# Rotary products of Strassen's queries issued one by one behind score tiles' maxima

## The chip, the cores and the metric

The kernel runs on one core of one Trainium2 chip. The metric is the device time of one execution in microseconds (us), as the median of the runs shown; the profile is of one further execution. The engines are called PE (matrix products), DVE (vector), ACT (scalar functions), POOL (GpSimd) and SP (issues most DMAs).

## The reference

One decoder layer on a sequence of 1024 rows of width 512, all in float32: attention with 32 query heads and 8 key/value heads of width 128, rotary positions and a causal mask, an output projection, layer normalisation, then a gated network of inner width 1792 and a second normalisation.

```python
q = (x @ wq).reshape(B, T, H, HD).transpose(0, 2, 1, 3)     # H = 32, HD = 128
k = (x @ wk).reshape(B, T, KV, HD).transpose(0, 2, 1, 3)    # KV = 8
v = (x @ wv).reshape(B, T, KV, HD).transpose(0, 2, 1, 3)
q = q * cos + _rotate_half(q) * sin
k = k * cos + _rotate_half(k) * sin
...
scores = jnp.einsum('bhtd,bhsd->bhts', q, k) * (1.0 / np.sqrt(HD))
scores = jnp.where(mask, scores, -jnp.inf)
att = jax.nn.softmax(scores, axis=-1)
out = jnp.einsum('bhts,bhsd->bhtd', att, v)
...
x = _layernorm(x + out @ wo, axis=-1)
x = _layernorm(x + ffn(x), axis=-1)
```

## The kernel before

The work runs over eight groups g. A group is one key/value head with its four query heads. Its 1024 rows are cut into eight row tiles i of 128 rows, taken in the order 7, 1, 5, 3, 4, 2, 6, 0: odd row tiles in the first half of a group, even ones in the second. Each row tile is cut again into four score tiles t = 4i to 4i + 3. A score tile holds 32 rows of all four heads and (t + 1) x 32 keys, so s_28 to s_31 are the long ones with which a group begins, and s_0 to s_3 the short ones with which it ends. The text calls the passage from s_3 of one group to s_28 of the next a turn.

**A score tile** (function scores). PE multiplies the rotated queries by the keys into one of two PSUM pairs (pool ps_s). DVE adds the mask and takes the row extreme in one instruction (L503; the profile calls its result low; the text calls it the tile's maximum). ACT takes the exponential (L517), which frees the PSUM pair. DVE takes the reciprocal of the sums (L521), ACT scales (L522), and DVE transposes in blocks (L525). After a row tile's fourth score tile, SP issues 16 DMAs (gather, L575) that complete the transposition; only then can PE form o, the weights times v (class Late, which also runs the output projection y of a pair of row tiles, with the sums os that POOL forms at L651 to L654 and the accumulation on DVE at L672).

**The next group's projections** (class Early) fill PE between score tiles: keys, values and queries of g + 1, in units of one 512-wide matmul. Most pairs of query heads, 13 of 16, are projected with Strassen's seven products (project_two, in the order 1, 2, 6, 5, 3, 7, 4), whose weight sums POOL forms ahead in weigh (L248 to L251). Four results come out: c11 and c12 are the odd row tiles of the pair's first and second head, c21 and c22 the even ones. The three other pairs (the list PLAIN) are projected directly.

**The rotation** (rotate) of one result takes three products on DVE, two of half the partitions with sin (L381) into a buffer rope_b, of which there are two, and one with cos in place (L387), and one add on POOL (L390). In project_two all four follow at once when the result is complete. The queries of odd rows of g + 1 must be complete, for all four heads, before s_28 of g + 1; those of even rows are first read at the fifth row tile.

**The order.** A scheduler orders instructions on each engine by the order in which they are written and by when it deems them ready; PE's order is the written one. The written order comes from a planner that counts PE's units: function run fills the time after each score tile with Late's steps that are due and else with Early's steps. For the groups 0 to 5 Early must be done EARLIER score tiles before a group's end:

```python
pace = early.total * min(1, passed / (slots - EARLIER))
must = early.total - MOST * max(0, slots - EARLIER - done)
```

The o of a row tile counts as ready to be used COPY = 5 units after its last matmul, so that y of that pair is written later. In the first group the residual rows x are loaded into sums (load_x, L292 to L300), with two memsets and a subtraction on POOL for each of four pairs of row tiles, and each weight block is turned into a difference on POOL (difference, L256) after its first use.

Of the kernel before, what the change touches and what calls it, by code (L numbers as in the profile page):

```python
# [35 lines left out]
P = 128  # L36
# [8 lines left out]
NT = T // P  # L45
# [40 lines left out]
STEP = 3.5  # L86
LAG = 7

EARLIER = 2

LEAST = 2

# [2 lines left out]
def kernel(  # L95
# [55 lines left out]
    def piece(name):  # L151
        return cp.tile([P, T], F32, tag="c", name=name)
# [27 lines left out]
    with ExitStack() as att:  # L180
# [108 lines left out]
        def load_x(k):  # L289


            for n in range(2):  # L292
                i = ORDER[2 * k + n]
                to = sums[k][:, 2:4, :] if n else sums[k][:, 1:7:5, :]
                src = x_in[i * P : (i + 1) * P, :]
                nc.sync.dma_start(to, src.rearrange("p (n f) -> p n f", n=2))
            a1, _, _, a5, a6, a7, a3 = (sums[k][:, n, :] for n in range(7))
            nc.gpsimd.memset(a1, 0.0)
            nc.gpsimd.memset(sums[k][:, 4:6, :], 0.0)
            nc.gpsimd.tensor_tensor(a3, a3, a5, ALU.subtract)  # L300
# [41 lines left out]
        nc.vector.tensor_tensor(s2, s1, a11, ALU.subtract)  # L342
        nc.vector.tensor_tensor(s4, a12, s2, ALU.subtract)

        def values(g, even):

            if g not in vs:
                vs[g] = piece(f"v{g}").rearrange("p (j f) -> p j f", j=NT)
            pv = mbank(f"v_ps{g}_{even}")
            for j in range(NT // 2):  # L350
                for c, (w, x) in enumerate(operands(wvs[g], even)):
                    matmul(
                        pv[:, j * HD : (j + 1) * HD],
                        lhsT=x[:, j * P : (j + 1) * P],
                        rhs=w,
                        start=(c == 0),
                        stop=(c == NC - 1),
                    )
                if j == NT // 2 - 1:
                    nc.scalar.copy(  # L360
                        vs[g][:, 1 - even :: 2, :], pv.rearrange("p (j f) -> p j f", f=HD)
                    )
                    if even:
                        load_wv(g + 1)
                    else:
                        difference(wvs[g])
                yield NC * HD / W

        def alike(t, dst):

            return t.rearrange("p (n q) -> p n q", q=dst.shape[-1])

        def rotate(dst, src, even, name):

            ts = slice(even * W, (even + 1) * W)
            b = ap.tile([P, W], F32, tag="rope_b", name=f"{name}_b{even}")


            def swapped():
                for to, of in ((slice(0, 64), slice(64, P)), (slice(64, P), slice(0, 64))):  # L380
                    nc.vector.tensor_tensor(  # L381
                        alike(b, dst)[to], src[of], alike(sin[:, ts], dst)[of], ALU.mult
                    )

            if src is dst:
                swapped()
            nc.vector.tensor_tensor(dst, src, alike(cos[:, ts], dst), ALU.mult)  # L387
            if src is not dst:
                swapped()
            nc.gpsimd.tensor_tensor(dst, dst, alike(b, dst), ALU.add)  # L390

        def project(dst, w, even, name):

            ps = mbank(f"{name}_ps{even}")
            for c, (w_c, x_c) in enumerate(operands(w, even)):
                matmul(ps, lhsT=w_c, rhs=x_c, start=(c == 0), stop=(c == NC - 1))
                if c < NC - 1:
                    yield 1
            rotate(dst, alike(ps, dst), even, name)
            if not even:  # L400
                difference(w)
            yield 1

# [7 lines left out]

        def project_queries(g, head, even):
            dst = queries(g, even)[:, :, head, :]
            yield from project(dst, wqs[g * REP + head], even, f"q{g}_{head}")
            if even and head % 2:
                for h in (head - 1, head):
                    load_wq((g + 1) * REP + h)
                weigh((g * REP + head) // 2 + 1)

        def project_two(g, n):  # L420


            b11, b21, b22, u1, u2, u3, u4 = sums_of[g * 2 + n]
            u = f"{g}_{n}"
            v = ap.tile([P, W], F32, tag="v", bufs=1, name=f"qv{u}")
            c11, c12, c21, c22 = (
                queries(g, even)[:, :, 2 * n + h, :] for even in range(2) for h in range(2)
            )
            v_q = alike(v, c11)
            ps = {}  # L430
            products = (
                (1, b11, a11), (2, b21, a12), (6, u2, s2), (5, u1, s1), (3, b22, s4),
                (7, u3, s3), (4, u4, a22),
            )
            for k, w, x in products:
                ps[k] = mbank(f"q{u}_p{k}")
                q = alike(ps[k], c11)
                for c in range(NC // 2):
                    matmul(
                        ps[k], lhsT=w[:, c], rhs=x[:, c], start=c == 0, stop=c == NC // 2 - 1  # L440
                    )
                    if c < NC // 2 - 1:
                        yield 1
                if k == 1:
                    nc.scalar.copy(v, ps[1])
                elif k == 2:
                    nc.vector.tensor_tensor(c11, q, v_q, ALU.add)
                    rotate(c11, c11, 0, f"q{u}_0")
                elif k == 6:
                    nc.vector.tensor_tensor(v, ps[6], v, ALU.add)  # L450
                elif k == 5:
                    nc.vector.tensor_tensor(c12, q, v_q, ALU.add)
                elif k == 7:
                    nc.vector.tensor_tensor(v, ps[7], v, ALU.add)
                    nc.vector.tensor_tensor(c22, alike(ps[5], c22), v_q, ALU.add)
                    rotate(c22, c22, 1, f"q{u}_1")
                elif k == 4:
                    nc.vector.tensor_tensor(c21, q, v_q, ALU.add)
                    rotate(c21, c21, 1, f"q{u}_0")
                    for h in range(2):  # L460
                        load_wq((g + 1) * REP + 2 * n + h)
                    weigh(g * 2 + n + 1)
                else:
                    nc.vector.tensor_tensor(c12, q, c12, ALU.add)
                    rotate(c12, c12, 0, f"q{u}_1")
                yield 1

        def projections(g):
# [15 lines left out]
        def scores(g, t, kT, x):  # L484

            nonlocal last_of_all
            n, i, b = (t + 1) * Q, t // B, t % B
            full = (i + 1) * P  # L490
            u = f"{g}_{t}"
            s = pair(f"s{u}")
            for k0 in range(0, n, W):
                k1 = min(n, k0 + W)
                matmul(
                    s[:, k0:k1],
                    lhsT=queries(g, i % 2 == 0)[:, i // 2 * B + b].rearrange("p h q -> p (h q)"),
                    rhs=kT[:, k0:k1],
                    start=True,
                    stop=True,  # L500
                )
            low = stat("low", f"low{u}")
            nc.vector.tensor_tensor_reduce(  # L503
                out=s[:, :n],
                in0=s[:, :n],
                in1=mask[:, T - n :],
                scale=1.0,
                scalar=MASKED,
                op0=ALU.add,
                op1=ALU.min,  # L510
                accum_out=low,
            )
            p = piece(f"p{u}")
            if n < full:
                nc.gpsimd.memset(p[:, n:full], 0.0)  # L515
            total = stat("total", f"total{u}")
            nc.scalar.activation(  # L517
                p[:, :n], s[:, :n], AF.Exp, bias=low, scale=-1.0, accum_out=total
            )
            share = stat("share", f"share{u}")  # L520
            nc.vector.reciprocal(share, total)  # L521
            last_of_all = nc.scalar.activation(p[:, :n], p[:, :n], AF.Copy, scale=share)  # L522
            if x is None:
                return p[:, :full]
            nc.vector.transpose(  # L525
                x[:, :, :, b, :].rearrange("p b j q -> p j b q"),
                p[:, :full].rearrange("p (j b k) -> p j b k", b=B, k=Q),
            )
# [326 lines left out]
        for g in range(KV):  # L855
# [21 lines left out]
            passed = 0.0  # L877
            due = now
            for p, i in enumerate(ORDER):
                if g == KV - 1 and p == 1:  # L880
                    load_wo(g)
                x = turned(g, p, i)
                unturned = []
                for b in range(B):
# [337 lines left out]
```

## Time and profile before

| | us |
|---|---|
| median of 3 runs | 1336.13 (1335.11 to 1337.87) |
| profiled execution | 1334.31 |
| its span, first to last instruction | 1332.4 |
| PE busy | 1283.2 |
| DVE busy | 830.4 |
| ACT busy | 466.1 |
| POOL busy | 421.2 |
| mean clock granted to PE | 0.986 of full |

A row of the timeline reads: start in us from the span's begin, length in us, engine, line and operation, output<-inputs, the shape, how many records were merged (a matmul in float32 leaves two), and in brackets the engine's idle time before it and what ended it. A row of the waits reads: total us, how many times, the longest. Line numbers such as L503 are those of the kernel before.

### The profile page before, as it was taken

How to read it: one execution, taken by the hardware profiler on the slowest of the kernel's cores; microseconds unless marked ns; L12 is line 12 of the kernel's file. 1: busy time of each engine (PE TensorE's matmuls, PEld its weight loads, DVE VectorE, ACT ScalarE, POOL GpSimd, SP SyncE). 2: the span in 40 equal slices, each digit the busy share in tenths (PEclk: the TensorE clock that was granted, in tenths of full speed). 3: DMA queues.
4: the chain of work that ended last, by engine and by line, in shares of the span. 5: the costliest groups of instructions: out<-in, count | busy, mean ns of one | idle time of the engine just before them, and what ended most of it. 6: DMA issues, size and time to landing. Idle time of an engine off the chain costs nothing. (4 is left out here: it accounts for less than half of the span.)

```text
span 1332.4 us, 13958 instructions
## 1 busy us (share of the span) xinstructions
PE 1283.2 (96%) x4046; PEld 719.8 (54%) x4046; DVE 830.4 (62%) x1665; ACT 466.1 (35%) x924; POOL 421.2 (32%) x631
## 2 busy tenths in 40 slices
PE   8999989998998999899999999999999999999998
PEld 3565555655564656465556565654655644444445
DVE  5567766776678667867676768686755564344122
ACT  0443344434443444344434344445445111111000
POOL 6233333332333233413332323252320534532000
PEclk9899989998999999999999999999999999999999
DMA  7243215342534243334333433433444611100000
GB/s 244 52 117 93 71 44 144 89 101 53 137 88 106 56 127 93 89 75 118 83 92 82 127 80 81 112 90 89 118 102 103 187 32 47 48 27 5 16 24 24
DMA packets 104235, 115.52 MB, mean 87 GB/s; under 512 B 19040, under 2 KB 79200, under 8 KB 104160
## 3 DMA queue, kind: packets, MB, share of 16 engines
q1 hardware_dynamic: 103152, 112.67, 32.4%
q10 hardware_dynamic: 1008, 1.97, 0.4%
q8 instruction: 33, 0.54, 0.2%
q14 instruction: 42, 0.34, 0.1%
HBM read 37.23 MB, written 2.10 MB: 30 GB/s over the span
## 5 line engine op out<-in xcount | busy, mean ns | idle before, releaser
L517 ACT ACTIVATE p<-s,low 128x928 f32<-128x928 f32 (+31 forms) x256 | 178.9, 699 | 463.7 <-DVE low L503 445.5
L134 PE MATMUL s<-kT,queries 128*128 128x512 f32 (+15 forms) x768 | 281.0, 476 | 37.2 <-ACT p L517 31.6
L134 PE MATMUL o<-moved,v 128*128 128x512 f32 x550 | 256.7, 598 | 0.2 <-issue 0.2
L134 PEld LDWEIGHTS s<-kT,queries 128*128 128x128 f32 x768 | 144.1, 193 | 193.2 <-issue 151.1
L525 DVE STREAM_TRANSPOSE turned<-p 128x1024 f32<-128x1024 f32 (+7 forms) x244 | 186.3, 774 | 98.2 <-ACT p L522 68.9
L503 DVE CUSTOM_DVE_ANT_0 s<-s,mask 128x928 f32<-128x928 f32 (+31 forms) x256 | 178.5, 698 | 66.4 <-PE s L134 65.7
L522 ACT ACTIVATE p<-p,share 128x928 f32<-128x928 f32 (+31 forms) x256 | 187.0, 735 | 91.1 <-DVE share L521 91.1
L134 PEld LDWEIGHTS o<-moved,v 128*128 128x128 f32 x550 | 101.9, 191 | 96.8 <-issue 90.9
L390 POOL TENSOR_TENSOR queries<-queries,q_b 128x512 f32<-128x512 f32 x64 | 83.6, 1306 | 153.4 <-DVE queries L387 69.9
L521 DVE RECIPROCAL share<-total 128x1 f32<-128x1 f32 x256 | 41.1, 161 | 113.6 <-ACT p L517 111.2
L134 PE MATMUL y<-wo,oT 128*128 128x256 f32 x428 | 106.1, 384 | 0.0
L134 PE MATMUL q_p<-blocks,wq 128*128 128x512 f32 x208 | 98.9, 594 | 0.0
L515 POOL MEMSET p<- 128x96 f32 (+2 forms) x192 | 26.3, 151 | 220.7 <-DVE turned L525 205.9
L381 DVE TENSOR_TENSOR q_b<-queries,sin 64x512 f32<-64x512 f32 x104 | 93.5, 899 | 3.0
L134 PEld LDWEIGHTS y<-wo,oT 128*128 128x128 f32 x428 | 81.9, 194 | 24.4 <-issue 10.9
L134 PE MATMUL q_p<-blocks,uq 128*128 128x512 f32 x156 | 75.9, 594 | 0.0
L134 PEld LDWEIGHTS v_ps<-wv,blocks 128*128 128x128 f32 x512 | 64.1, 194 | 13.9 <-issue 11.2
L672 DVE TENSOR_TENSOR sums<-y,sums 128x512 f32<-128x512 f32 x112 | 67.9, 610 | 4.5 <-PE y L134 3.6
L134 PE MATMUL v_ps<-wv,blocks 128*128 128x128 f32 x512 | 64.5, 277 | 0.4 <-POOL p L515 0.4
L134 PE MATMUL f<-wd,hT 128*128 128x512 f32 (+1 forms) x162 | 64.8, 545 | 0.0
L134 PE MATMUL k_ps<-blocks,wk 128*128 128x512 f32 x128 | 62.8, 607 | 2.0 <-POOL wk L256 2.0
L134 PEld LDWEIGHTS q_p<-blocks,wq 128*128 128x128 f32 x208 | 38.7, 190 | 38.6 <-issue 35.4
(183 smaller groups left out, 1504.0 us busy)
## 6 DMA issues: line engine op xcount, KB each, us to landing
moved<-turned SPq DMA_DIRECT2D x112, 128.0 KB, 2.4
moved<-turned SPq DMA_DIRECT2D x128, 112.0 KB, 2.2
moved<-turned SPq DMA_DIRECT2D x112, 96.0 KB, 2.1
moved<-turned SPq DMA_DIRECT2D x112, 80.0 KB, 2.1
wq<-wq SPq DMA_DIRECT2D x32, 256.0 KB, 2.9
wo<-wo SPq DMA_DIRECT2D x32, 256.0 KB, 3.4
moved<-turned SPq DMA_DIRECT2D x128, 64.0 KB, 2.0
moved<-turned SPq DMA_DIRECT2D x128, 48.0 KB, 1.9
```

The source lines that it names most:

```text
L134: tc.keep_in_program_order(nc.tensor.matmul(*args, **kw))
L381: nc.vector.tensor_tensor(alike(b, dst)[to], src[of], alike(sin[:, ts], dst)[of], ALU.mult)
L390: nc.gpsimd.tensor_tensor(dst, dst, alike(b, dst), ALU.add)
L503: nc.vector.tensor_tensor_reduce(out=s[:, :n], in0=s[:, :n], in1=mask[:, T - n :], scale=1.0, scalar=MASKED, op0=ALU.add, op1=ALU.min, acc ...
L515: nc.gpsimd.memset(p[:, n:full], 0.0)
L517: nc.scalar.activation(p[:, :n], s[:, :n], AF.Exp, bias=low, scale=-1.0, accum_out=total)
L521: nc.vector.reciprocal(share, total)
L522: last_of_all = nc.scalar.activation(p[:, :n], p[:, :n], AF.Copy, scale=share)
L525: nc.vector.transpose(x[:, :, :, b, :].rearrange("p b j q -> p j b q"), p[:, :full].rearrange("p (j b k) -> p j b k", b=B, k=Q),)
L672: pin(nc.vector.tensor_tensor(to, out, to, ALU.add))
```

## The change

Three things are edited. In project_two the calls of rotate become rotate_later: each puts three pieces of work, the two half products and the cos product with its add, into one of two queues (chores), one for odd and one for even row tiles. The function chore takes the next piece, odd rows' rotations first and each rotation to its end, and scores calls it once behind each tile's maximum, twice for the short tiles of row tile 0. Before a group's first score tile what is left for odd rows is written out; before its fifth row tile, everything. EARLIER goes from 2 to 3. In the first group the memsets and subtractions of load_x become begin_sums, written ahead of the first four row tiles one pair at a time, and the four weight differences of the first queries are written ahead of the first row tile.

```diff
-EARLIER = 2
+EARLIER = 3
...
+        def begin_sums(k):
             a1, _, _, a5, a6, a7, a3 = (sums[k][:, n, :] for n in range(7))
             nc.gpsimd.memset(a1, 0.0)
             nc.gpsimd.memset(sums[k][:, 4:6, :], 0.0)
...
+        chores = deque(), deque()
+
+        def rotate_later(dst, even, name):
+
+            ts = slice(even * W, (even + 1) * W)
+            b = []
+
+            def half(to, of):
+                if not b:
+                    b.append(ap.tile([P, W], F32, tag="rope_b", name=f"{name}_b{even}"))
+                nc.vector.tensor_tensor(
+                    alike(b[0], dst)[to], dst[of], alike(sin[:, ts], dst)[of], ALU.mult
+                )
+
+            def whole():
+                nc.vector.tensor_tensor(dst, dst, alike(cos[:, ts], dst), ALU.mult)
+                nc.gpsimd.tensor_tensor(dst, dst, alike(b[0], dst), ALU.add)
+
+            low, high = slice(0, 64), slice(64, P)
+            chores[even].extend([lambda: half(low, high), lambda: half(high, low), whole])
+
+        def chore(behind=None):
+
+
+            nonlocal current
+            if current is None:
+                current = next((c for c in chores if c), None)
+            if current is None:
+                return False
+            with tc.issue_after(behind) if behind is not None else ExitStack():
+                current.popleft()()
+            if len(current) % 3 == 0:
+                current = None
+            return True
...
-            if not even:
+            if not even and diff:
                 difference(w)
...
                 elif k == 2:
                     nc.vector.tensor_tensor(c11, q, v_q, ALU.add)
-                    rotate(c11, c11, 0, f"q{u}_0")
+                    rotate_later(c11, 0, f"q{u}_0")
...
-                    rotate(c22, c22, 1, f"q{u}_1")
+                    rotate_later(c22, 1, f"q{u}_1")
...
-                    rotate(c21, c21, 1, f"q{u}_0")
+                    rotate_later(c21, 1, f"q{u}_0")
...
-                    rotate(c12, c12, 0, f"q{u}_1")
+                    rotate_later(c12, 0, f"q{u}_1")
...
-            nc.vector.tensor_tensor_reduce(
+            extreme = nc.vector.tensor_tensor_reduce(
...
+            for _ in range(2 if i == 0 else 1):
+                chore(extreme.ins)
...
             for p, i in enumerate(ORDER):
+                while p % 4 == 0 and (chores[0] or (p and chores[1])):
+                    chore()
                 if g == KV - 1 and p == 1:
                     load_wo(g)
+                if g == 0 and p == 0:
+                    for a in range(REP):
+                        difference(wqs[a])
+                if g == 0 and p < NT // 2:
+                    begin_sums(p)
```

More of the change, by code (lines that the diff above doesn't have):

```diff
@@ L383, in swapped, with project @@
                     )
-            if src is dst:
-                swapped()
             nc.vector.tensor_tensor(dst, src, alike(cos[:, ts], dst), ALU.mult)
-            if src is not dst:
-                swapped()
+            swapped()
             nc.gpsimd.tensor_tensor(dst, dst, alike(b, dst), ALU.add)
-        def project(dst, w, even, name):
+        chores = deque(), deque()
[22 more added lines that the diff above has]
+            if len(current) % 3 == 0:
+                current = None
+            return True
+        def project(dst, w, even, name, diff=True):
             ps = mbank(f"{name}_ps{even}")
@@ L413, in project_queries @@
             dst = queries(g, even)[:, :, head, :]
-            yield from project(dst, wqs[g * REP + head], even, f"q{g}_{head}")
+            yield from project(dst, wqs[g * REP + head], even, f"q{g}_{head}", g > 0)
             if even and head % 2:
```

## Prediction

> **What bounds the kernel now.** I read the page's busy table first, then the waits of PE, then PE's timeline around the long waits, then DVE and POOL over the same stretch.
>
> ```profile
> PE 1283.2 (96%) x4046; PEld 719.8 (54%) x4046; DVE 830.4 (62%) x1665; ACT 466.1 (35%) x924; POOL 421.2 (32%) x631
> ```
>
> PE is the bound: 1283.2 of 1332.4 us busy, so 49.2 us idle, and the change adds and removes no matmul. It can win only what lies in those 49.2 us (and in PE's slow-clock time), and loses whatever idle time it creates. PE's waits (total us, times, longest us):
>
> ```profile
> PE s L134 <- ACT p L517: 31.6, 15, 5.0
> PE s L134 <- POOL queries L390: 5.0, 1, 5.0
> ```
>
> A score tile's product waits until the exponential of the tile two before has emptied its PSUM pair: 31.6 us. PE's timeline (start, us, ..., idle before) shows where:
>
> ```profile
> 157.61 0.30 PE L134 MATMUL s<-kT,queries 128*128 128x32 f32 x2
> 157.75 1.10 PE L134 MATMUL o<-moved,v 128*128 128x512 f32 x2
> ...
> 166.31 0.49 PE L134 MATMUL s<-kT,queries 128*128 128x128 f32 x2
> 166.63 1.89 PE L134 MATMUL y<-u,os 128*128 128x256 f32 x8
> 173.48 3.43 PE L134 MATMUL s<-kT,queries 128*128 128x512 f32 x4 [4.96 <-ACT p L517]
> 176.71 1.57 PE L134 MATMUL y<-wo,oT 128*128 128x256 f32 x4
> 178.11 1.03 PE L134 MATMUL y<-wo,os 128*128 128x256 f32 x4
> ```
> ```profile
> 303.35 3.43 PE L134 MATMUL s<-kT,queries 128*128 128x512 f32 x4 [4.96 <-ACT p L517]
> ```
> ```profile
> 562.73 2.68 PE L134 MATMUL s<-kT,queries 128*128 128x512 f32 x4 [4.10 <-ACT p L517]
> ```
> ```profile
> 689.92 1.79 PE L134 MATMUL s<-kT,queries 128*128 128x512 f32 x4 [1.96 <-ACT p L517]
> ```
>
> These are the turns from one group to the next, between the four short tiles s_0 to s_3 and the long s_28: six turns, idle 4.96, 4.96, 5.22 (0.27 and 4.95 at 433), 4.10, 1.96, 1.97 (at 817), in all 23.2 us. After a long one the same form of s_28 takes 3.43 instead of 1.79 and the next y 1.57 (1.03 warm): the clock has fallen. That loses 2.2, 2.1, 1.7 and 1.7 us at the first four. A turn now costs 31 us over all six. The cause is on DVE:
>
> ```profile
> 165.62 0.14 DVE L503 DVE_READ_ACCUMULATOR2_ANT low<- 128x1 f32 x1
> 165.78 2.20 DVE L381 TENSOR_TENSOR q_b<-queries,sin 64x512 f32<-64x512 f32 x2
> ...
> 170.04 2.56 DVE L381 TENSOR_TENSOR q_b<-queries,sin 64x512 f32<-64x512 f32 x2
> 172.52 0.25 DVE L503 CUSTOM_DVE_ANT_0 s<-s,mask 128x96 f32<-128x96 f32 x1
> ```
>
> Between the maxima of s_1 and s_2 lie 6.8 us of rotary products. And POOL:
>
> ```profile
> 159.75 0.72 POOL L651 TENSOR_TENSOR os<-oT 128x256 f32<-128x256 f32 x1
> ...
> 161.91 1.18 POOL L654 TENSOR_TENSOR os<-oT,os 128x256 f32<-128x256 f32 x1
> 165.04 1.26 POOL L390 TENSOR_TENSOR queries<-queries,q_b 128x512 f32<-128x512 f32 x1 [1.95 <-DMA moved<-turned]
> 166.26 1.18 POOL L248 TENSOR_TENSOR uq<-wq,wq 128x256 f32<-128x256 f32 x1
> ...
> 169.33 1.06 POOL L251 TENSOR_TENSOR uq<-wq,uq 128x256 f32<-128x256 f32 x1
> 170.35 1.70 POOL L390 TENSOR_TENSOR queries<-queries,q_b 128x512 f32<-128x512 f32 x1
> ```
>
> The add at 165.04 is the last one that s_28 needs (odd tiles, second head); it stands ahead of weigh's four subtractions (L248 to L251), so POOL is not what PE waits for here.
>
> **The change: rotations behind maxima.** Counts stay: 52 rotations of three DVE products and one POOL add. What changes is their place. In the instruction order of the changed program DVE has one product (two at the short tiles) behind each maximum, odd tiles' rotations first. Between the maxima of s_1 and s_2 only one half product and a reciprocal remain, 1.3 us for 6.8. That takes away the wait shown. But the same order shows two new things at every one of the six turns.
>
> First, EARLIER = 3: the projections are all spent one tile sooner. PE has the output product o of tile row 2, the two matmuls of the pair's last product (4), then s_1, s_2, s_3 and s_28 with nothing between them. Before, 2.6, 1.7 and 1.7 us of q_p and y matmuls stood there; they now stand behind s_28 and can't cover a wait of s_28.
>
> Second, the add of that second odd rotation now comes late: on POOL it stands behind os (L651 to L654), the add of the first odd rotation, and weigh's four. POOL runs in order, so s_28 waits for all of it. From the end of o (158.85 in the trace of before) on: 0.90 to the first os (ACT's copy between, 159.75), os 3.34 (to 163.09), add 1.26, weigh 4.13 (166.26 to 170.39), add 1.26 to 1.70 (both rows are there; I take the middle, 1.48), and 0.05 to PE's start (the add that ended at 36.05 and PE's start at 36.10). Sum 11.16 us. PE has in that time 1.72 for two matmuls and 0.17 + 0.20 + 0.32 for s_1 to s_3: 2.41. Idle 8.75 us a turn. At the first turn weigh's first subtraction stands before the other add; the sum is the same.
>
> Is DVE later than that? From the same zero: tile 27's transposition ended 6.94 after its product began (152.67 to 159.61), 0.65 of it a product of v that now stands behind; the o ends 6.8 after that start (1.5 for s_27, five matmuls of 0.86, s_0, one more), so the transposition ends at -0.5, v takes 0.65 and the maximum of s_0 0.30, done at about 0.5. Then 0.68 (c22), 1.12 (cos beside a busy POOL), 1.15 (half of 2.2 to 2.4), 0.16, 0.67, 0.30, 0.36 (s_1), 1.15, 0.16, 0.35 (s_2), 1.12 (cos of the odd rotation): 7.7. POOL reaches the add at 9.6, so POOL decides by 1.9 us. The exponential of s_2 is done by 7.2. Without weigh in the way the add would end at 9.1, idle 6.7.
>
> **The clock.** The row first: after idle of 4.96, s_28 and y lost 2.2 us; after 1.96, none (1.79 for s_28). The Trainium skill, "TensorE: Matmul & The Clock Gate", Part 1, says PE falls to half clock after an idle window of about 3.4 us and comes back only after a busy one, the windows running freely. It speaks against this change: two turns that pay nothing today would pay, and the penalty would be half of 3.4 to 6.8 us, 1.7 to 3.4 a turn, 10 to 20 in all; by the row, 6 x 2.2 = 13. I use the row, and the rule's ends for the range.
>
> New cost of the turns: 6 x (8.75 + 2.2) = 65.7, less today's 31: +34.7 us.
>
> **Elsewhere in a group.** The wait that moves on: the transposition of tile 31 (L525) now has a half product in front of it, 1.15 us later at most, and its 16 DMAs are what o of row 7 waits for. In the trace it ended at 197.99; 16 issues of 0.63 and 2.4 to land give 210.4, the o matmul began at 212.75. The new order puts that o one tile later, so it stays covered. In short tiles 4 to 7 PE has 2.2 to 2.5 us each where DVE needs about 2.2; between 0 and +6 over six groups, below nothing -1.9, which is all that waits of 0.3 to 0.6 in mid group hold. I take +1. On SP one wq load of a pair (0.5 us to issue, and a wait for PE) moves ahead of row 6's gather; that gather has over 10 us to spare before its o, as s_28 to s_30, y and k_ps now come first. ACT keeps its work.
>
> **GpSimd's first group.** In the built order the eight memsets and four subtractions of sums stand where they stood; only the first wq difference (L256) passes the memsets. POOL then waits 3.75 us for wo until 17.32 anyway, which covers it; the 5.01 us at 36.10 and 1.99 at 20.54 on PE stay, since every add and difference around them keeps its place. Without that cover it would cost the 2.9 us of memsets. I take 0; a gain of more than 2 is excluded, as nothing on POOL in front of those adds goes away. The other three differences keep their place too.
>
> **Sum.** 1332.4 + 34.7 + 1 = 1368.1 span. The profiled execution took 1334.31, 1.9 above its span, and stands 1.8 under the median of 1336.13: 1371.8.
>
> **The rivals.** (a) Faster: the tile chain alone decides. If the odd adds land early, s_28 waits only for the exponential of s_2; with half products at the undisturbed 0.69 that is t = 5.8 on the scale above, idle 3.4 and little slow clock: 6 x 3.4 = 20.4 for 31, about -10.6 us, 1325.5. It decides from the point where idle and slow clock stay under 5.2 us a turn, that is, the last add landed by about 7.6. For it: DVE's gap shrinks from 6.8 to 1.3. Against it: POOL's queue shows 8.7 us of work in front of that add after 0.9. 8 in 100.
>
> (b) Slower, but less: os or weigh run earlier than I place them, and DVE's 9.1 decides: 6 x (6.7 + 2.2) - 31 = +22, 1359. 10 in 100.
>
> (c) Slower, and more: longer slow clock (3.4) and o waiting for gathers in mid group: 6 x (9.5 + 3.4) - 31 + 6 = +52, 1389. 10 in 100.
>
> (d) The change doing nothing, as its GpSimd part does in the built order: gains and losses at the turns cancel. The different PE order at all six turns speaks against it: 2 in 100.
>
> The likeliest case has 70 in 100. A measurement of this kernel tells 0.2%, 2.7 us, from no change. Faster 0.08, same 0.02, slower 0.90. The range: the main case runs from +28 to +49 (add 1.26 or 1.70, clock 1.7 to 3.4, mid group -2 to +6), and (b) and part of (c) are taken in: 1352 to 1391.
>
> **What would show it.** Right: at the six turns PE's s_28 waits for POOL queries, 8 to 10 us in two pieces around s_3 (the first for ACT p), in all 48 to 60 us; s_28 at 3 us or more; busy sums unchanged; PE idle near 85 us. Wrong: PE's wait for ACT p gone with no wait for POOL in its place; or the wait for POOL near 4, then weigh ran ahead; or new waits of o for DMA.

## The result, and the profile after

The changed kernel takes 1380.51 us (median of 4 runs, 1379.3 to 1381.53); the kernel before, run beside it, 1335.62 (4 runs, 1334.97 to 1337.87). The ratio is 1.0333, interval 1.0315 to 1.0351: 45 us slower. The profiled execution took 1381.53 with a span of 1379.8, 47.4 longer than the span before, at a mean granted PE clock of 0.971 (0.986 before).

The page's busy table of the changed kernel:

```profile
PE 1289.6 (93%) x4046; PEld 722.3 (52%) x4046; DVE 823.5 (60%) x1665; ACT 466.8 (34%) x924; POOL 423.8 (31%) x631
```

The work is the same, instruction for instruction in number. PE is idle for 1379.8 - 1289.6 = 90.2 us, 41.0 more than before, and busy 6.4 longer. Its waits (us in all, times, longest):

```profile
PE s L134 <- POOL queries L411: 43.2, 6, 7.3
PE s L134 <- ACT p L558: 20.9, 17, 2.5
PE s L134 <- POOL queries L391: 6.7, 1, 6.7
PE q_p L134 <- DVE sums L713: 6.3, 5, 1.4
```

The first row is new: score products wait for the rotated queries that POOL's add writes (L390 of before is L411 here in project_two's rotations, and L391 in the direct ones). It stands at six places, once in each turn. PE's timeline at the first turn (start, us, idle before in brackets), and then the matching lines of the second:

```profile
160.08 1.10 PE L134 MATMUL o<-moved,v 128*128 128x512 f32 x2
161.02 1.88 PE L134 MATMUL q_p<-blocks,uq 128*128 128x512 f32 x4
162.74 0.58 PE L134 MATMUL s<-kT,queries 128*128 128x64 f32 x4
165.84 0.77 PE L134 MATMUL s<-kT,queries 128*128 128x128 f32 x2 [2.52 <-ACT p L558]
173.50 3.46 PE L134 MATMUL s<-kT,queries 128*128 128x512 f32 x4 [6.88 <-POOL queries L411]
176.75 3.28 PE L134 MATMUL y<-wo,oT 128*128 128x256 f32 x8
179.86 1.03 PE L134 MATMUL y<-u,oT 128*128 128x256 f32 x4
...
302.81 0.49 PE L134 MATMUL s<-kT,queries 128*128 128x128 f32 x2 [2.06 <-ACT p L558]
310.56 3.46 PE L134 MATMUL s<-kT,queries 128*128 128x512 f32 x4 [7.26 <-POOL queries L411]
```

Between o and s_28 stand only the last product's two matmuls (inside the q_p row) and s_1 to s_3. PE idles 2.52 + 6.88 = 9.40 us at this turn and 9.30 to 9.32 at the other five (2.05 or 2.06, and 7.25 or 7.26), 56.0 in all where the kernel before had 23.2. Then s_28 takes 3.46 us and the eight y records after it 3.28, at half speed; the next y is back at 1.03 for four. At the later turns these eight y records take less (3.01 at the second turn, 1.89 at the sixth).

DVE over the first turn:

```profile
165.16 0.13 DVE L541 DVE_READ_ACCUMULATOR2_ANT low<- 128x1 f32 x1
165.32 1.92 DVE L405 TENSOR_TENSOR q_b<-queries,sin 64x512 f32<-64x512 f32 x2
167.27 0.16 DVE L562 RECIPROCAL share<-total 128x1 f32<-128x1 f32 x1
167.35 0.25 DVE L541 CUSTOM_DVE_ANT_0 s<-s,mask 128x96 f32<-128x96 f32 x1
167.52 1.39 DVE L410 TENSOR_TENSOR queries<-queries,cos 128x512 f32<-128x512 f32 x1
```

The 6.8 us of rotary products between the maxima of s_1 and s_2 have shrunk to about 2.1 (165.29 to 167.35): the change does what it says. And DVE has finished the odd rotation's last product (cos, in place) at 168.91. POOL:

```profile
161.89 0.73 POOL L692 TENSOR_TENSOR os<-oT 128x256 f32<-128x256 f32 x1 [1.09 <-ACT oT L790]
...
164.84 0.72 POOL L695 TENSOR_TENSOR os<-oT,os 128x256 f32<-128x256 f32 x1
165.52 1.17 POOL L248 TENSOR_TENSOR uq<-wq,wq 128x256 f32<-128x256 f32 x1
166.66 1.70 POOL L411 TENSOR_TENSOR queries<-queries,q_b 128x512 f32<-128x512 f32 x1
168.32 1.17 POOL L249 TENSOR_TENSOR wq<-wq 128x256 f32<-128x256 f32 x1
169.45 1.17 POOL L250 TENSOR_TENSOR uq<-wq,uq 128x256 f32<-128x256 f32 x1
170.70 1.08 POOL L251 TENSOR_TENSOR uq<-wq,uq 128x256 f32<-128x256 f32 x1
171.74 1.70 POOL L411 TENSOR_TENSOR queries<-queries,q_b 128x512 f32<-128x512 f32 x1
```

The add that s_28 needs runs from 171.74 to 173.44, and s_28 starts at 173.50. Its inputs had been ready since 168.91. For the 2.8 us between, POOL worked on weigh's last three subtractions, which nobody on PE waits for at that time. The first turn is the exception: at the other five, all four subtractions stand in front of that add, and its inputs are ready 5.2 us before POOL gets to it. At the second turn:

```profile
303.25 0.86 DVE L410 TENSOR_TENSOR queries<-queries,cos 128x512 f32<-128x512 f32 x1
...
309.26 1.25 POOL L411 TENSOR_TENSOR queries<-queries,q_b 128x512 f32<-128x512 f32 x1
```

### The profile page after: what moved, and what is told of

It is laid out like the page before. It is cut to its first block, busy times and chain, and to the rows that moved or that the text cites. A ratio compares the mean times of both kernels' runs of the same rounds, so it can differ in the third digit from the quotient of the medians.

```text
span 1379.8 us, 13917 instructions
## 1 busy us (share of the span) xinstructions
PE 1289.6 (93%) x4046; PEld 722.3 (52%) x4046; DVE 823.5 (60%) x1665; ACT 466.8 (34%) x924; POOL 423.8 (31%) x631
## 3 DMA queue, kind: packets, MB, share of 16 engines
q10 hardware_dynamic: 1008, 1.97, 0.4%
## 5 line engine op out<-in xcount | busy, mean ns | idle before, releaser
L134 PE MATMUL s<-kT,queries 128*128 128x512 f32 (+15 forms) x768 | 285.9, 484 | 71.0 <-POOL queries L411 43.2
L411 POOL TENSOR_TENSOR queries<-queries,q_b 128x512 f32<-128x512 f32 x52 | 73.1, 1406 | 150.2 <-DVE queries L410 138.0
L405 DVE TENSOR_TENSOR q_b<-queries,sin 64x512 f32<-64x512 f32 x104 | 81.1, 780 | 15.5 <-POOL queries L411 12.6
L790 ACT COPY oT<-o 128x512 f32<-128x512 f32 x58 | 33.8, 582 | 75.0 <-PE o L134 74.2
```

The source lines that it names most:

```text
L134: tc.keep_in_program_order(nc.tensor.matmul(*args, **kw))
L405: nc.vector.tensor_tensor(alike(b[0], dst)[to], dst[of], alike(sin[:, ts], dst)[of], ALU.mult)
L411: nc.gpsimd.tensor_tensor(dst, dst, alike(b[0], dst), ALU.add)
L790: nc.scalar.copy(oT, o)
```

## The experiments

Every kernel here computes the whole reference. Each is given by its difference from the kernel that it starts from, and its ratio is to the kernel before. The kernel before was measured again beside them: 1335.62 us beside the changed kernel, 1334.39 beside the first four experiments, 1333.86 beside the others. So a difference in us between kernels of different rounds is uncertain by 1 to 2. Two questions: which of the change's edits costs the time, and through what.

**One number back.** The changed kernel with

```diff
-EARLIER = 3
+EARLIER = 2
```

> The changed kernel with EARLIER back at 2, nothing else. Theory A (the turn lost its cover: with EARLIER = 3 no matmul is left between s_1, s_2, s_3 and s_28, and s_28 waits for POOL's add behind os and weigh): from the end of o, PE now has about 9.3 us of work before s_28 (three q_p matmuls, s_1, 2.6, s_2, 1.7, s_3, 1.7), POOL's add ends near 11 (weigh from 5.3, when product 4 is done, 4.1, then the add 1.5); idle about 2 us a turn, no slow clock: 6 x 2 = 12 us at the turns for the 31 of before, so about 1320 us, between 1312 and 1330. Theory B (the pieces behind the maxima delay the tiles, whatever PE has between them): stays slow, above 1365 us.

Measured: 1305.92 us, ratio 0.9788 (0.9773 to 0.9802), faster by more than expected. Busy table, the wait, and PE at the second turn:

```profile
PE 1269.7 (97%) x4046; PEld 714.6 (55%) x4046; DVE 819.5 (63%) x1665; ACT 468.4 (36%) x924; POOL 416.6 (32%) x631
```
```profile
PE s L134 <- POOL queries L411: 7.0, 6, 3.2
```
```profile
292.11 1.89 PE L134 MATMUL y<-u,os 128*128 128x256 f32 x8
295.25 1.82 PE L134 MATMUL s<-kT,queries 128*128 128x512 f32 x4 [1.25 <-POOL queries L411]
```

With y standing between s_3 and s_28 again, s_28 still waits for the same add at all six turns, but 0.3 to 3.2 us of it are left, 7.0 in all. s_28 takes 1.82 or 1.83 at all six turns, so none of these waits was followed by the slow clock. PE is idle for 33.8 us instead of 49.2, and busy for 1269.7 instead of 1283.2. So the rotary pieces make the kernel faster, by 28 us, and the one number turns that into a loss of 45.

**The number alone.** The kernel before with

```diff
-EARLIER = 2
+EARLIER = 3
```

> The kernel before with EARLIER = 3, nothing else: all of a rotation's products at once, as before. Theory A: the cover is gone here too; on DVE s_1 and s_2 stand behind whole rotations, so s_2's exponential ends some 13 us after the end of o where PE has 2.4 us of work: idle 9 to 11 us a turn, ended by ACT p and not by POOL, with slow clock 3: 6 x 13 = 78 for 31, about 1380 us, between 1368 and 1392. Theory B (the pieces cost the time): as before, 1336 us.

Measured: 1365.5 us, ratio 1.0233 (1.0216 to 1.025). Slower with the releaser expected, by less than expected. Its wait row, and PE at the first turn:

```profile
PE s L134 <- ACT p L517: 55.0, 27, 5.9
```
```profile
164.87 0.46 PE L134 MATMUL s<-kT,queries 128*128 128x96 f32 x2 [1.38 <-ACT p L517]
171.25 0.80 PE L134 MATMUL s<-kT,queries 128*128 128x128 f32 x2 [5.92 <-ACT p L517]
172.51 3.43 PE L134 MATMUL s<-kT,queries 128*128 128x512 f32 x4 [0.46 <-ACT p L517]
```

The turn idles 1.38 + 5.92 + 0.46 = 7.76 us: without the y in between, PE runs into DVE's rotary products one tile sooner (here they fill most of the 6.0 us between the maxima of s_0 and s_1, 164.34 to 170.38). So the number costs 31 us where the old rotations stand, and 1380.51 - 1305.92 = 75 us where the new ones stand. The two edits are not additive: +31 and -28 alone, +45 together. What EARLIER = 3 takes away is the cover, that is, the PE work that fills the time until s_28 may start. The pieces need it more, because in their order the last add comes late: s_28 starts 11.9 to 12.3 us after the end of o in the changed kernel, 10.9 in this run. Beside that, only the two edits together bring a wait of q_p (below).

**weigh behind the add.** In the changed kernel, weigh's four subtractions are kept back until the odd rotations are done, and issued behind the last odd add:

```diff
-                    weigh(g * 2 + n + 1)
+                    held_weighs.append(g * 2 + n + 1)
+                    weigh_behind()
...
+        def weigh_behind():
+            if held_weighs and not chores[0] and (current is not chores[0]):
+                with tc.issue_after(last_odd[0].ins):
+                    weigh(held_weighs.popleft())
```

(weigh_behind is also called at the end of chore; whole records the add of an odd rotation in last_odd.)

> The changed kernel, with POOL's four weight subtractions of weigh held until the pair's second odd rotation is added; PE's and DVE's orders are the same. Theory A (s_28 waits for POOL's queue): in the changed kernel's profile the cos product of that rotation ended at 168.9 and the add at 173.4; without weigh in between the add ends near 170.4, so 3 us less a turn, wait for POOL 4 to 4.5 instead of 7.2: 18 us less, about 1362 us, between 1358 and 1368. Rival (the tile chain over DVE and ACT holds s_28, the add being only the last to arrive): less than 6 us gained, 1375 or more.

Measured: 1357.57 us, ratio 1.0166 (1.015 to 1.0182), 23 us less than the changed kernel and a little more gained than expected. The wait row, and s_28 at the second turn:

```profile
PE s L134 <- POOL queries L417: 19.7, 6, 3.8
```
```profile
301.95 3.46 PE L134 MATMUL s<-kT,queries 128*128 128x512 f32 x4 [3.18 <-POOL queries L417]
```

The wait falls from 7.26 to 3.18 at this turn and from 43.2 to 19.7 in all, 23.5 us, which is the whole gain (the spans differ by 23.7). This shows that POOL's order set the end of the turn: the orders of PE, DVE and ACT in the trace are those of the changed kernel, instruction for instruction. The rest of the wait (os and two adds) stays, and so does the slow clock: though the last wait is about half as long, s_28 still takes 3.40 to 3.46.

**GpSimd's part alone.** The kernel before with only the edits for the first group:

```diff
+        def begin_sums(k):
...
-            if not even:
+            if not even and diff:
                 difference(w)
...
+                if g == 0 and p == 0:
+                    for a in range(REP):
+                        difference(wqs[a])
+                if g == 0 and p < NT // 2:
+                    begin_sums(p)
```

> The kernel before with only the GpSimd part of the change (memsets, subtractions and weight differences of the first group written later). Theory: the built order hardly changes and POOL waits for wo anyway; 1336 us, within 2. Rival: part of the 45 us comes from the start, then 2 to 6 us slower with a longer wait of s_28 for POOL queries at 36 us.

Measured: 1335.69 us, ratio 1.0004 (0.9994 to 1.0014): no change. The start is as it was (before: 5.0 at 36.10):

```profile
36.16 3.46 PE L134 MATMUL s<-kT,queries 128*128 128x512 f32 x4 [5.02 <-POOL queries L392]
```

**The clock.** The changed kernel with 14 matmuls whose result nobody reads, put in front of s_28 in groups 1 to 6, so that PE works through the wait:

```diff
+                if 0 < g < KV - 1 and p == 0:
+                    warm = mbank(f"warm{g}")[:, : 2 * P]
+                    for _ in range(14):
+                        matmul(warm, lhsT=ident, rhs=cos[:, : 2 * P])
```

> The changed kernel (EARLIER = 3) with 14 matmuls of 128x256 that nobody reads between s_3 and s_28 at the six turns, 14 x 0.43 = 6.0 us warm, to stand in the wait of 7.26. Theory (clock): s_28 and the y behind it run at full clock again, so PE's busy time without the added matmuls falls by 6 x 3.1 = 18 us while POOL still sets when s_28 starts: about 1362 us, between 1358 and 1368. Rival (the long s_28 has another cause, such as late reads of the queries): no change, 1378 to 1384, or slower if the added matmuls outlast the wait.

Measured: 1367.45 us, ratio 1.0251 (1.0235 to 1.0266): faster than the changed kernel by added work, by 13 us as the times stand and by 11 as the ratios do. The second turn:

```profile
301.13 6.21 PE L134 MATMUL warm<-cos,ident 128*128 128x256 f32 x28
308.59 1.82 PE L134 MATMUL s<-kT,queries 128*128 128x512 f32 x4 [1.25 <-POOL queries L411]
310.25 1.89 PE L134 MATMUL y<-wo,oT 128*128 128x256 f32 x8
```

At this turn and two others POOL still sets the start of s_28; at the other three the added matmuls end last, 0.3 to 0.4 us later. At all six, s_28 takes 1.72 to 1.82 for 3.34 to 3.46, and y 1.89. The added matmuls take 42.2 us, which at their ends overlap a little with other matmuls. Every moment counted once, PE's other work takes 1275.0 us, that is 14.6 less than in the changed kernel. The rest of the span, idle or added work, is 1366.3 - 1275.0 = 91.3 us, 1.1 more than the 90.2 of idle. So the waits alone keep their cost, and what follows from them on the clock is about 15 us. I had expected 18.

**Both remedies.** The changed kernel with EARLIER = 2 and weigh behind the odd add, that is, the first and the third edit together.

> The changed kernel with EARLIER = 2 and weigh behind the pair's odd adds, both edits together. With EARLIER = 2 alone PE still waited 7.0 us for POOL queries over the six turns (3.2 at the first), with weigh's four subtractions in front of the add. Theory A (POOL's queue): in the turn at 295 us of that run the cos product ended at 292.3 and the add could then end at 293.5, before PE is through with y at 294.0; so these 7 us go to below 2 and the time is about 1300 us, between 1297 and 1303. Rival (the wait passes on to ACT p or to a later use of weigh's sums): 1305 to 1308, as with EARLIER = 2 alone.

Measured: 1299.37 us, ratio 0.974 (0.9726 to 0.9755), as expected. It is the fastest version found, 2.6% under the kernel before. The wait for queries at the turns is down to one:

```profile
PE s L134 <- POOL queries L417: 1.3, 1, 1.3
```

PE is busy for 1269.4 of 1296.9 us, 98%.

**One less still.** The changed kernel with

```diff
-EARLIER = 3
+EARLIER = 1
```

> The changed kernel with EARLIER = 1. Theory A (each step of EARLIER trades cover for the time at which the last odd rotation is ready): PE has more work between the short tiles, but product 3, which the last odd rotation needs, comes about 1.7 us later than with EARLIER = 2, and its pieces then stand behind s_2 and s_3: idle 2 to 5 us a turn, 1308 to 1325 us, slower than EARLIER = 2 and faster than 3. Rival (only cover counts): below 1304.

Measured: 1309.42 us, ratio 0.9815 (0.9798 to 0.9831). The time lies at the low end of what was expected, but not in the way expected:

```profile
PE s L134 <- POOL queries L411: 6.9, 2, 3.6
```

Only the first two turns wait, the other four not at all. At those two turns s_28 takes 3.27 and 3.30, at the others 1.72. So once there is some PE work between s_3 and s_28, how much matters little: 1306 with 2 and 1309 with 1, against 1381 with none (3).

**Whole rotations behind one maximum.** The changed kernel with EARLIER = 2, and the three products of a rotation taken together behind one maximum instead of one by one:

```diff
-            chores[even].extend([lambda: half(low, high), lambda: half(high, low), whole])
+            def all_three():
+                half(low, high)
+                half(high, low)
+                whole()
+            chores[even].append(all_three)
...
-            if len(current) % 3 == 0:
-                current = None
+            current = None
...
-            for _ in range(2 if i == 0 else 1):
-                chore(extreme.ins)
+            chore(extreme.ins)
```

> The changed kernel with EARLIER = 2 and each rotation put whole (two half products and cos) behind one maximum, one at a time, odd rows first. If the gain over the kernel before comes from rotations standing behind a maximum instead of in front of it, most of it stays: 1304 to 1314. If it comes from taking the products one by one, most of it goes: 1320 or more, with s waiting for ACT p again at the turns.

Measured: 1306.79 us, ratio 0.9796 (0.9782 to 0.9811), against 0.9788 (0.9773 to 0.9802) with single products. The intervals overlap nearly whole. The gain of the rotary edit is that rotations wait behind maxima, one rotation to a maximum and odd tiles first; cutting them into products adds nothing that these runs can tell. (All of this is with EARLIER = 2; with 3 it was not run.)

## Why the prediction was right, and where its sizes were off

**Sign, place and cause were right.** The forecast was 1372 with 1352 to 1391, and 1380.5 lies inside. The signs it named stand in the trace: six waits for POOL's queries, in two pieces around s_3 with the first for ACT, 8 to 10 us (9.3 to 9.4), s_28 above 3 us (3.46), PE idle near 85 (90.2). The add stands where the prediction put it, behind os, the first odd add and weigh, and DVE is done 2.8 us before POOL gets there at the first turn and 5.2 at the others (predicted 1.9).

**The chain of a turn was 0.8 to 1.2 us too short.** From the end of o to s_28 the prediction has 11.16 us. Measured are 12.3 at the first turn and 11.94 at the other five. The terms, each until the next begins:

| | predicted | first turn | second turn |
|---|---|---|---|
| until the first os | 0.90 | 0.70 | 0.71 |
| os | 3.34 | 3.64 | 4.20 |
| first add | 1.26 | 1.66 | 1.66 |
| weigh | 4.13 | 4.56 | 4.07 |
| last add, and to PE's start | 1.53 | 1.75 | 1.30 |

The row of the first add is 1.70 at all six turns, where the low one of the two durations in the trace of before (1.26 and 1.70) was taken. The last add, put at the middle, is 1.70 at the first turn and 1.25 at the other five. At these five the largest miss is os. PE's own work in that time was 2.92 at the first turn (s_3 alone took 0.77, partly at the low clock) and 2.63 at the others instead of 2.41, so only part of the difference became idle: 9.40 and 9.31 for 8.75, and 56.0 in all for 52.5.

**The slow clock was sized nearly right.** The sum had 2.2 us a turn, 13 in all, from the row after 4.96 of idle. Measured, s_28 loses 3.46 - 1.79 = 1.67 at each turn (1.55 at the sixth). The eight y records behind it, 1.89 at full clock, lose 1.39 at the first turn, then 1.12, 0.80, 0.76, 0.27 and nothing. That is 3.06 at the first turn, 1.55 at the last, and 14.2 over six. The second and the sixth turn:

```profile
313.82 3.01 PE L134 MATMUL y<-wo,oT 128*128 128x256 f32 x8
...
859.13 3.34 PE L134 MATMUL s<-kT,queries 128*128 128x512 f32 x4 [7.25 <-POOL queries L411]
862.30 1.89 PE L134 MATMUL y<-wo,oT 128*128 128x256 f32 x8
```

The granted clock shows why the turns differ. A row gives a stretch from s_28's start, its length, PE's busy time and matmuls, the granted clock, and the DMAs' share and GB/s:

```profile
310.56:316.08 5.52, 5.52 (x10) 0.50 0.00 0
859.13:862.22 3.09, 3.09 (x4) 0.50 0.00 0
```

In the clock records both low stretches begin during the wait and last 10.24 us; at 316.08 and 862.22 the clock is back at 1.00. Half of what is left of them when s_28 starts, 2.76 and 1.55 us, is what these turns lose (2.79 and 1.55). From the second turn to the sixth the low stretches begin 136.5 us apart and the s_28 on average 137.1, so s_28 meets a shorter rest each time. The estimate from the rule of the Trainium skill weighed there ("TensorE: Matmul & The Clock Gate", Part 1; 1.7 to 3.4 us a turn) holds five of the six values, and the sixth lies just below; the row and the rule were both fair guides. The matmuls that fill the wait show the wait as the cause: 14.6 us of PE time came back. Turns together: 56.0 + 14.2 = 70.2 for the 65.7 of the sum.

**The middle of a group was sized at +1 and gave about +7.6 of idle.** This is the largest miss of the sum. The prediction had short tiles 4 to 7 at 0 to +6 and chose +1. Half a microsecond at s_7 came in most groups, as waits for ACT. What was not in the sum at all is a wait of the last Strassen products:

```profile
381.89 1.12 PE L134 MATMUL q_p<-blocks,uq 128*128 128x512 f32 x2 [1.41 <-DVE sums L713]
```

Five times, 6.3 us. DVE just before it:

```profile
379.77 0.69 DVE L405 TENSOR_TENSOR q_b<-queries,sin 64x512 f32<-64x512 f32 x1
380.49 0.69 DVE L410 TENSOR_TENSOR queries<-queries,cos 128x512 f32<-128x512 f32 x1
381.10 0.15 DVE L562 RECIPROCAL share<-total 128x1 f32<-128x1 f32 x1
381.17 0.67 DVE L713 TENSOR_TENSOR sums<-y,sums 128x512 f32<-128x512 f32 x1
```

The accumulation that reads y stands behind two rotary products, and q_p starts when it is done. The wait is also there with weigh moved (5.8) and with the filling matmuls (5.4), and it is absent with EARLIER = 2 and in the kernel before with EARLIER = 3. It needs both edits: rotary products in front of the accumulation, and q_p early enough to want that space. That it is the PSUM space of y that q_p waits for fits the releaser named, but no run separates it.

**GpSimd's first group was rightly put at nothing**, by the trace and by the run of that part alone. In the changed kernel the waits at the start are 6.7 for 5.0 and 2.5 for 2.0, but s_28 begins at 36.13 for 36.10. The kernel before with EARLIER = 3 alone has the 6.7 as well, so it isn't the GpSimd edit's; PE only gets there sooner.

**The account.** Idle: turns +32.8, middle +7.6, the last groups -1.6, start +2.2, in all the measured 41.0. Busy: the slow clock at the turns adds 14.2 - 7.7 = 6.5, s_3 of the first turn 0.3, and the start gives 1.6 back (four k_ps records in 1.98 us for 3.58), which makes +5.2 where +6.4 was measured; 1.2 is not placed.

**The rivals.** (a), the tile chain relieved and the kernel faster, described a real effect: with EARLIER = 2 it is worth 28 us. In the changed kernel it fails at the point that the prediction gave: the last add lands about 12 us after o, not 7.6. (b), weigh not in the way, is close to the kernel with weigh moved: its wait was put at 6.7 a turn (5.2 at the second turn, 2.06 and 3.18) and its time at 1359 (1357.6). That the times agree so well is partly luck: the shorter waits are made up for by those of q_p, which (b) did not count. Where the prediction was blind is the split: it judged the change as one, did not ask what each edit was worth without the other, and so did not say that one number carries the whole loss.

## What to carry to other kernels

Issuing filling work one step earlier can remove the only work that stood between two dependent tiles on the bound engine: before moving it, list what is left between them and set it against the latest input. On an engine that works in order, look at what is queued in front of that input; here four subtractions that nobody needed yet, moved behind one add, were worth 23 us with the cover gone and 6.5 us with it there. And when a change has several edits, price each with the others left out as well: +31 and -28 became +45.

## What was not expected of the hardware

After waits of 7 us PE runs at half speed over more than the one tile: at the first turn s_28 and the eight y records behind it take 3.46 and 3.28 us for 1.79 and 1.89. How much is lost does not follow from the length of the wait alone. With weigh moved, waits of 2.06 and 3.18 us around s_3 (2.52 and 3.79 at the first turn) cost as much clock as those of 2.06 and 7.26 in the changed kernel: 15.4 us over six turns against 14.2. With EARLIER = 2 a single wait of 3.18 cost no clock (s_28 in 1.82). With whole rotations s_28 took 1.82 after a wait of 1.97 at the second turn and 2.83 after the same 1.97 at the third, where the granted clock is 0.50 from 418.8 to 422.1. PE had no other idle time in the 13 us before, so here the clock fell without the idle window of about 3.4 us that the rule above asks for; the measurement decides. And adding 42 us of useless matmuls in the waits made the kernel 11 to 13 us faster.

POOL's 128x512 add takes 1.25 to 1.28 us or about 1.7. In the changed kernel's trace all 17 long ones overlap one of DVE's rotary products by 0.55 us or more, and 42 of the 47 short ones overlap none. In the trace of before, short ones overlap such products too, by up to 1.24 us, so the overlap alone does not decide. On DVE the half product took 0.69 in the middle of a group and two of them 1.92 beside POOL's subtraction and add.
